# Four layers of convolutions on one core: scan additions that wait for one engine alone, sums for two batches in one GpSimd instruction, two blocks of columns assembled ahead of a turn

## The chip, the cores and the metric

The kernel runs on one core of one Trainium2 chip. The metric is device time in microseconds (us) of one execution; lower is better. The core has TensorE (matmul), VectorE, ScalarE and GpSimd for computing and SyncE (SP), whose queue issues nearly all DMA transfers of this kernel; the profile calls them PE, DVE, ACT, POOL and SP. Each engine works through a queue of its own, and they meet through semaphores.

## The reference

The input is 4 batches of 48 channels of 256 x 256 float32. Four layers follow, each normalized by groups before and added to its input after. The first two (an attention with 3 x 3 convolutions, and a gated convolution) are not touched by the change. Layers 2 and 3 are the scans:

```python
def step(w, b):
    def f(carry, inp):
        nxt = inp + _conv1d(carry, w, b)   # 48 x 48 channels, 5 taps
        return (nxt, nxt)
    return f
# down over the rows, up over the results of down, then
# right over the columns of that, left over the results of right
_, d_rest = jax.lax.scan(step(down_w, down_b), d0, xs[1:])
_, u_rest = jax.lax.scan(step(down_w, down_b), u0, seq)
_, r_rest = jax.lax.scan(step(right_w, right_b), r0, ws[1:])
_, l_rest = jax.lax.scan(step(left_w, left_b), l0, R[Ww - 2::-1])
...
x = x + _L2_conv_ref(_gn(x), ...)
x = x + _L3_conv_ref(_gn(x), ...)
```

Every row or column needs the one before it, so a scan is a chain of 256 steps, and a layer has four of them.

## The kernel before, in words

The function `scans` holds both layers. The four batches are two pairs, and each pair is a **chain** (a Python generator, `chain(pair)`), which runs layer 2 and then layer 3 through down, up, right and left. A row or column of a pair lies on 96 partitions (2 neighbouring places of 48 channels) with 2 batches of 128 numbers, so that the 5 taps become 3 matmuls of 96 x 96 by 96 x 128.

A **step** (L1035 and after) takes the two batches in turn. For each it issues 3 float32 matmuls from the old carry into a bank of PSUM (L1045; the trace records each matmul as two), then one VectorE addition of the bank and the step's input into the new carry (L1049, or L1053 where the input is in one piece), and then calls `keep` for that batch. There are four carry buffers per chain, used in turn; a buffer is written again four steps after its last use. What `keep` does depends on the pass:

- down (L1127) and up (L1168): ScalarE writes the carry with a bias over the input row, in its place;
- right (L1248): ScalarE writes the carry with a bias into the buffer `lines`;
- left (L1293): GpSimd adds the carry to `stage`, which holds the layer's input, so that `stage` becomes the layer's output. In the last left pass of all (layer 3 of chain 1, called `direct`) GpSimd writes the sum into `done` (L1297) in the output's own layout, and SP's queue writes that out (L1316).

Rows are held in tiles of 32 (`RT`), columns in blocks of 16 (`CB`). Large buffers (`slot`) come from a ring of five per pair. While a tile is worked on, the next one is loaded; four ScalarE instructions (L1104, "norms") normalize it in the second half of a tile of the down pass. Results of down and of right go to DRAM (`D`, `Rt`) and come back for up and left; results of up go to `U` by rows and come back by columns (`col`). In right, GpSimd copies a column out of `col` into `pre` (`fetch`, L1225) three steps ahead. The first block of columns is needed as soon as the up pass ends, so it is assembled by hand: its rows from the older tiles are loaded from `U` (L1158) when the up pass is 24 rows into its last tile, and the newest rows are copied straight from the row buffers (L1180) and from `last` (L1192). The second block is loaded from `U` in one transfer (L1235) at the first step of right.

In left of layer 2, statistics for the next normalization are taken from each finished `stage` by eight VectorE instructions (L1325), which the source spreads over the next block's steps.

The order of the work is set by the generators: chain 0 runs alone for LEAD = 992 steps (most of its layer 2), then the chains take turns step by step until chain 0 ends, then chain 1 runs alone. A framework records the instructions, takes each engine's order from the recorded priorities and from its own estimate of when an instruction becomes ready, and adds the semaphore waits that the data need. A wait that an engine has already made, or a later one on the same semaphore, is not made again. An instruction with several waits gets instructions ahead of it that only wait; they show in the profile as EVENT_SEMAPHORE.

When chain 0 has ended, `to_rows(0)` brings its output from the scans' layout into that of the result while chain 1 runs alone: loads (`oi`), four copies for each of 16 halves of a block (`oo`, three on GpSimd at L1393 and one on ScalarE at L1395) and a write. The list `times` says at which of chain 1's steps each piece is issued.

Of the kernel before, what the change touches and what calls it, by code (L numbers as in the profile page):

```python
# [9 lines left out]
F32 = mybir.dt.float32  # L10
# [954 lines left out]
def scans(ctx, tc, xs, out, wts, biases, dram, k, coefs, lead, spare):  # L965
# [49 lines left out]
    def chain(pair):  # L1015
# [66 lines left out]
        def layer_of(layer, first):  # L1082
# [32 lines left out]
            for n in range(NT):  # L1115
                ahead_ = None
                for r in range(RT):
                    if r == 0 and n + 1 < NT:
                        ahead_ = [slot("dn"), slot("dn")]
                        load_rows(layer, n + 1, ahead_, 0, NK)  # L1120
                    if ahead_ and r >= RT // 2 and r % 4 == 0:
# [17 lines left out]


            nc.scalar.activation(last, inner(), AF.Identity, bias=bias[:, 0:1])
            column = None
            for n in reversed(range(NT)):
                ahead_ = None
                for r in reversed(range(RT)):
                    if r == RT - 1 and n > 0:
                        ahead_ = [slot("up"), slot("up")]
                        for i in range(2):
                            nc.sync.dma_start(ahead_[i], D[n - 1][i])
                    if n == 0 and r == RT // 4:  # L1150

                        column = slot("col")
                        v = cols_view(column)
                        for par in range(2):
                            for b in range(2):
                                h0 = NH + 1 - par
                                here = slice(par * C, (par + 1) * C)
                                nc.sync.dma_start(  # L1158
                                    v[here, b, :, h0:, :].rearrange("c q h w -> c q (h w)"),
                                    U[here, b, 0:2, h0:, :].rearrange("c q h w -> c q (h w)"),  # L1160
                                )
# [12 lines left out]
                    yield  # L1174
                    if n == 0 and r < 2:

                        par, h0 = 1 - r, r
                        v = cols_view(column)
                        for q in range(2):
                            nc.sync.dma_start(  # L1180
                                v[par * C : (par + 1) * C, :, q, h0 : h0 + NH, :].rearrange("c b h w -> c b (h w)"),
                                rows_view(now[r])[q * C : (q + 1) * C, :, 0].rearrange("c b h w -> c b (h w)"),
                            )
                if n == 0:

                    def keep(new, b):
                        nc.scalar.activation(last[:, b], new[:, b], AF.Identity, bias=bias[:, 1:2])

                    step(layer, 0, blocks(last), keep)
                    yield  # L1190
                    for q in range(2):
                        nc.sync.dma_start(cols_view(column)[0:C, :, q, 0, :], last[q * C : (q + 1) * C, :, 0:KC])  # L1192
                for r in range(2):
                    v = rows_view(now[r])
                    par = 1 - r
# [25 lines left out]
            def fetch(block, n, w):  # L1221
# [3 lines left out]
                nc.gpsimd.tensor_copy(t, cols_view(block)[:, :, w % 2, :, w // 2])  # L1225
                fetched[g] = t

            for w in range(1, 3):
# [36 lines left out]
            if layer == 0:  # L1265
                stats = [wp.tile([P, NK * 4, 6], F32, tag=f"st{pair}{b}", name="st") for b in range(2)]
            following = None

            direct = layer == 1 and pair == NP - 1
            done, width = None, 0
            writes = []
            for n in reversed(range(NK)):
                ahead_ = None
                if direct and n < 2:
                    done, width = take(0, "done").rearrange("p (b n) -> b p n", b=2), CB
                elif direct and n % 2 == 1:
                    done, width = [take(0, "done") for _ in range(2)], 2 * CB
                for w in reversed(range(CB)):  # L1280
                    if w == CB - 1 and n > 0:
                        ahead_ = slot("lines"), slot("stage")
# [7 lines left out]

                    def keep(new, b):
                        if not direct:
                            nc.gpsimd.tensor_add(to[:, b], to[:, b], new[:, b])  # L1293
                            return
                        for i in range(b.start, b.stop):
                            place = done[i].rearrange("p (h w) -> p h w", w=width)[:, :, n * CB % width + w]
                            nc.gpsimd.tensor_add(place, to[:, i], new[:, i])  # L1297

                    if n == NK - 1 and w == CB - 1:
                        keep(inner(), slice(0, 2))  # L1300
                    else:
                        step(layer, 2, line, keep)
                    if late:
                        late.pop(0)()
                    if writes and (w % 4 == 0 if n < 2 else w % 8 == 4):
                        writes.pop(0)()
                    yield
                if not direct:
                    nc.sync.dma_start(block_of(y, n), by_batch(stage))
                elif n * CB % width == 0:  # L1310

                    def write(b, r, done=done, width=width, w0=n * CB):
# [3 lines left out]
                        nc.sync.dma_start(  # L1316
                            at_rows[:, :, r, w0 : w0 + width],
                            done[b][r * C : (r + 1) * C].rearrange("c (h w) -> c h w", w=width),
                        )

                    writes += [lambda b=b, r=r, f=write: f(b, r) for b in range(2) for r in range(2)]
# [44 lines left out]
                    following = got  # L1366
            first = following

    def to_rows(pair):

        y = xs[2][pair]
        nh = SLOT // W
# [1 line left out]
        for n in range(H // 2 // nh):  # L1374
# [10 lines left out]
            for half in range(2):  # L1385
# [21 lines left out]
    while next(chains[0], True) is None:  # L1407
        next(chains[1])

    pieces = to_rows(0)  # L1410
# [129 lines left out]
```

## Time and profile before

| | us |
|---|---|
| median of 3 runs | 9103.32 |
| lowest and highest run | 9092.42 and 9108.16 |
| the profiled execution's own time | 9095.42 |
| its span, first to last instruction | 9093.6 |
| mean granted TensorE clock | 0.982 |

| stage of the profiled execution | from about, us |
|---|---|
| layers 0 and 1 | 0 |
| chain 0 alone: down, up, right of layer 2 | 3543, 3895, 4205 |
| chain 0 alone: left of layer 2 (few steps of chain 1 between) | 4575 |
| both chains: layer 3 of chain 0, layer 2 of chain 1 | 4986 |
| both chains in left | 6980 |
| chain 1 alone: down, up, right of layer 3 | 7640, 8010, 8317 |
| chain 1 alone: left of layer 3, written straight to the output | 8690 |
| last addition; after it only writes | 9049 |

How to read the profile: durations of single instructions are in ns, all else in us. A row of the costliest groups gives the line, engine and operation, output<-inputs by the program's names, shapes and count, then busy time, mean ns of one, and after the second bar the idle time of the engine just before them with what ended it. The table by stretches gives busy time and count for each engine in each stretch, then the granted TensorE clock, the share of the 16 DMA engines and GB/s. The chain of waits lists, in order of time, start, duration and what was worked on.

### The profile page before, as it was taken

To read this page: it belongs to the slowest core of one execution; us is meant where nothing else is said; L and a number is where in the kernel's file an instruction comes from. 1 tells how busy PE (TensorE), PEld (TensorE's weight loads), DVE (VectorE), ACT (ScalarE), POOL (GpSimd) and SP (SyncE) were. 2 spreads that over 40 slices of the span, in tenths; PEclk is the share of its full clock that TensorE was granted. 3 is DMA by queue.
4 is the path that set the end of the run, shared out by engine and by line. 5 is a ranking of instruction groups with operands and counts; after the bars stand their busy time and mean duration, and the time that the engine had idled before them with its cause. 6 is when DMAs were issued, how large, how long until landed. Compare 5 with 4: busy or idle time off the path is not lost.

```text
span 9093.6 us, 162344 instructions
## 1 busy us (share of the span) xinstructions
PE 8711.1 (96%) x62920; PEld 7268.3 (80%) x62920; DVE 3759.8 (41%) x10790; ACT 3489.6 (38%) x7033; POOL 2067.0 (23%) x3855
## 2 busy tenths in 40 slices
PE   6999999999999987999999999999999999999997
PEld 4777777433333345999999999999999999999997
DVE  3332010234555555444455444444445554343443
ACT  0011000123343355755511776665662004665510
POOL 0000000001111120002465000002446773002475
PEclk9999999999999988999999999999999999999998
DMA  7663323467878878655587773656556787888689
GB/s 150 132 135 87 74 59 73 97 136 168 181 171 187 177 165 165 149 133 128 145 211 178 157 147 95 160 129 160 154 152 177 218 227 169 172 183 201 175 173 168
DMA packets 1201990, 1390.61 MB, mean 153 GB/s; under 512 B 285712, under 2 KB 1128208, under 8 KB 1138240
## 3 DMA queue, kind: packets, MB, share of 16 engines
q1 hardware_dynamic: 1201120, 1379.90, 67.3%
q8 instruction: 493, 8.08, 0.4%
q14 instruction: 281, 2.30, 0.1%
q0 software_dynamic: 96, 0.33, 0.0%
HBM read 812.02 MB, written 509.61 MB: 145 GB/s over the span
## 4 chain that ended last, share of the span: by engine, by line
PE 88%; DMA 4%; DVE 3%; ACT 1%; issue 1%; SPq 1%; POOL 1%; DVEq 0%; POOLq 0%; ACTq 0%
PE ps L1045 57%; PE py L581 7%; PE acc L294 6%; PE acc L295 5%; PE acc L296 4%; PE py L590 3%; PE pt L276 1%; DMA stage<-x 1%; DMA tok<-x 1%; PE ph L698 1%; PE pout L868 1%; DMA x<-y 1%; PE ptok L751 1%; ACT x1n L541 1%; DMA sx<-in_x 1%
## 5 line engine op out<-in xcount | busy, mean ns | idle before, releaser
L1045 PE MATMUL ps<-carry,w 96*96 96x128 f32 x48960 | 5496.1, 275 | 75.6 <-DVE carry L1049 29.7
L1045 PEld LDWEIGHTS ps<-carry,w 96*96 96x96 f32 x48960 | 5445.9, 163 | 129.1 <-DVE carry L1053 39.6
L1225 POOL COPY pre<-col 96x256 f32<-96x256 f32 x1020 | 655.1, 644 | 2800.1 <-DMA col<-last 2011.7
L1248 ACT ACTIVATE lines<-carry,b 96x128 f32<-96x128 f32 (+1 forms) x2044 | 817.0, 402 | 618.8 <-DVE carry L1053 615.2
L1127 ACT ACTIVATE dn<-carry,b 96x128 f32<-96x128 f32 (+1 forms) x2044 | 770.1, 398 | 712.0 <-DVE carry L1049 709.2
L1049 DVE TENSOR_TENSOR carry<-ps,dn 96x128 f32<-96x128 f32 x2280 | 654.7, 288 | 900.5 <-PE ps L1045 806.8
L1053 DVE TENSOR_TENSOR carry<-ps,pre 96x128 f32<-96x128 f32 x2040 | 586.1, 287 | 798.7 <-PE ps L1045 544.8
L1168 ACT ACTIVATE up<-carry,b 96x128 f32<-96x128 f32 x1792 | 718.1, 402 | 480.1 <-DVE carry L1049 479.0
L1293 POOL TENSOR_TENSOR stage<-stage,carry 96x128 f32<-96x128 f32 (+1 forms) x1533 | 790.7, 519 | 314.2 <-DVE carry L1053 184.3
L1053 DVE TENSOR_TENSOR carry<-ps,lines 96x128 f32<-96x128 f32 x2040 | 576.2, 286 | 671.8 <-PE ps L1045 636.8
L1049 DVE TENSOR_TENSOR carry<-ps,up 96x128 f32<-96x128 f32 x1792 | 515.8, 288 | 678.9 <-PE ps L1045 667.9
L581 PE MATMUL py<-x1n,wy 128*96 128x512 f32 x1536 | 705.2, 609 | 29.1 <-ACT x1n L541 27.9
L295 PE MATMUL acc<-xs,xt 128*96 128x288 f32 x2048 | 666.4, 407 | 0.0
L294 PE MATMUL acc<-xt 128*96 128x288 f32 x2048 | 665.9, 408 | 0.0
L581 PEld LDWEIGHTS py<-x1n,wy 128*96 128x96 f32 x1536 | 245.2, 166 | 453.4 <-issue 436.1
L261 ACT ACTIVATE xn<-raw,coef 96x2048 f32<-96x2048 f32 x64 | 133.6, 2093 | 985.8 <-PE pt L276 818.2
L296 PE MATMUL acc<-xt,xs 128*96 128x192 f32 x2048 | 501.8, 327 | 0.0
L279 DVE COPY xt<-pt 128x384 f32<-128x384 f32 x256 | 136.5, 554 | 848.1 <-PE pt L276 649.4
L296 PEld LDWEIGHTS acc<-xt,xs 128*96 128x96 f32 x2048 | 332.0, 164 | 154.2 <-issue 1.2
L295 PEld LDWEIGHTS acc<-xs,xt 128*96 128x96 f32 x2048 | 331.8, 164 | 151.0 <-issue 2.0
L604 DVE TENSOR_TENSOR y<-py,t 96x512 f32<-96x512 f32 x256 | 171.4, 678 | 596.8 <-PE py L590 596.8
L590 PE MATMUL py<-x2n,wy 64*96 64x512 f32 x1536 | 363.0, 601 | 0.0
(179 smaller groups left out, 4823.8 us busy)
## 6 DMA issues: line engine op xcount, KB each, us to landing
stage<-x SPq DMA_DIRECT2D x64, 1536.0 KB
dn<-x SPq DMA_DIRECT2D x240, 384.0 KB
col<-U SPq DMA_DIRECT2D x60, 1536.0 KB
R<-lines SPq DMA_DIRECT2D x60, 1536.0 KB
lines<-R SPq DMA_DIRECT2D x60, 1536.0 KB
D<-dn SPq DMA_DIRECT2D x56, 1536.0 KB
up<-D SPq DMA_DIRECT2D x56, 1536.0 KB
U<-up SPq DMA_DIRECT2D x224, 384.0 KB
```

The lines of the kernel that those rows point to most:

```text
L294: nc.tensor.matmul(acc[0], lhsT=xt[:, h + 2, :], rhs=xt[:, here, :], start=first, stop=last)
L295: nc.tensor.matmul(acc[1], lhsT=xt[:, h + 2, :], rhs=xs[:, here, :], start=first, stop=last)
L296: nc.tensor.matmul(acc[2], lhsT=xs[:, h + 2, :], rhs=xt[:, past, :], start=first, stop=last)
L581: nc.tensor.matmul(ps, lhsT=held["w"][0][:, dx], rhs=x1n[:, 2 * c : 2 * c + 2, dx : dx + W], start=dx == 0, stop=False)
L1045: nc.tensor.matmul(ps, lhsT=w_sb[layer][:, way, j, :], rhs=old[:, i, j : j + W // 2], start=j == 0, stop=j == 2)
L1049: nc.vector.tensor_add(new[:, i].rearrange("p (k w) -> p k w", w=KC), ps.rearrange("p (k w) -> p k w", w=KC), inp[:, i])
L1053: nc.vector.tensor_add(new[:, i], ps, inp[:, i])
L1127: nc.scalar.activation(inp[:, b], blocks(new[:, b]), AF.Identity, bias=bias[:, 0:1])
L1168: nc.scalar.activation(place[:, b], blocks(new[:, b]), AF.Identity, bias=bias[:, 1:2])
L1225: nc.gpsimd.tensor_copy(t, cols_view(block)[:, :, w % 2, :, w // 2])
L1248: nc.scalar.activation(line[:, b], new[:, b], AF.Identity, bias=bias[:, 2:3])
L1293: nc.gpsimd.tensor_add(to[:, b], to[:, b], new[:, b])
```

## The change

Four things change, all of them in `scans`.

1. A new helper `look` is called after each step. It keeps the place that `keep` wrote in this step, and when more than three are kept it takes the oldest and has VectorE read one of its numbers into `seen` (in right together with one number of a fetched column). The list is cleared at the start of every tile of down and up, of right and of left. The last left pass does not call it.
2. In left, other than the last left pass, the GpSimd sum is made once for both batches, after the second addition.
3. At the turn from up to right the second block of columns is assembled by hand as the first was: loads from `U`, copies from the row buffers and from `last`, for two blocks each.
4. In the last left pass, blocks 1 and 0 are collected in one pair of `done` buffers like all others and written together, 32 columns wide, where each was written by itself before. In `to_rows`, the fourth copy is on GpSimd for the pieces up to the sixteenth time and on ScalarE after it, and the last eight times move from 508 + 28 i to 530 + 24 i.

```diff
+        seen = wp.tile([P, 1], F32, tag=f"seen{pair}", name="seen")
+        kept = []
+
+        def look(place, fetched=None):
+            kept.append(place)
+            if len(kept) > 3:
+                if fetched is None:
+                    nc.vector.tensor_copy(seen, kept.pop(0))
+                else:
+                    nc.vector.tensor_add(seen, kept.pop(0), fetched)
...
                     else:
                         step(layer, 0, inp, keep)
+                    look(inp[:, 1, 0, 0:1])
...
-                        column = slot("col")
-                        v = cols_view(column)
-                        for par in range(2):
-                            for b in range(2):
...
-                                    U[here, b, 0:2, h0:, :].rearrange("c q h w -> c q (h w)"),
+                        columns = [slot("col") for _ in range(2)]
+                        for j in range(2):
+                            v = cols_view(columns[j])
+                            for par in range(2):
+                                for b in range(2):
...
+                                        U[here, b, 2 * j : 2 * j + 2, h0:, :].rearrange("c q h w -> c q (h w)"),
...
                         step(layer, 0, place, keep)
+                    look(place[:, 1, 0, 0:1])
...
-                    if w == 0 and n + 1 < NK:
+                    if w == 0 and n == 0:
+                        ahead_ = columns[1]
+                    elif w == 0 and n + 1 < NK:
...
                         step(layer, 1, fetched.pop(n * CB + w), keep)
+                    if n + 1 < NK or w + 1 < CB:
+                        look(line[:, 1, 0:1], fetched[n * CB + w + 1][:, 1, 0:1])
...
-                if direct and n < 2:
-                    done, width = take(0, "done").rearrange("p (b n) -> b p n", b=2), CB
-                elif direct and n % 2 == 1:
-                    done, width = [take(0, "done") for _ in range(2)], 2 * CB
+                if direct and n % 2 == 1:
+                    done = [take(0, "done") for _ in range(2)]
...
                         if not direct:
-                            nc.gpsimd.tensor_add(to[:, b], to[:, b], new[:, b])
+                            if b.stop == 2:
+                                nc.gpsimd.tensor_add(to, to, new)
                             return
...
                         step(layer, 2, line, keep)
+                    if not direct:
+                        look(to[:, 1, 0:1])
...
-                    if writes and (w % 4 == 0 if n < 2 else w % 8 == 4):
+                    if writes and w % 8 == 4:
                         writes.pop(0)()
...
-                    if i < 3:
-                        nc.gpsimd.tensor_copy(dst, src)
+                    if engines[i] is nc.scalar:
+                        nc.scalar.copy(dst, src)
                     else:
-                        nc.scalar.copy(dst, src)
+                        engines[i].tensor_copy(dst, src)
...
-    times = [20 + 26 * i for i in range(16)] + [508 + 28 * i for i in range(8)]
+    times = [20 + 26 * i for i in range(16)] + [530 + 24 * i for i in range(8)]
     for i, _ in enumerate(chains[1]):
+        if i == times[16]:
+            engines[3] = nc.scalar
```

In the changed kernel the reads of `look` stand at lines 1035 and 1037, the matmuls at 1060, the additions at 1064 and 1068, and the GpSimd sum of left at 1325.

More of the change, by code (lines that the diff above doesn't have):

```diff
@@ L1120, in layer_of @@
                         load_rows(layer, n + 1, ahead_, 0, NK)
+                    if r == 0:
+                        kept.clear()
                     if ahead_ and r >= RT // 2 and r % 4 == 0:
@@ L1141, in layer_of @@
             nc.scalar.activation(last, inner(), AF.Identity, bias=bias[:, 0:1])
-            column = None
+            columns = None
             for n in reversed(range(NT)):
                 ahead_ = None
+                kept.clear()
                 for r in reversed(range(RT)):
@@ L1150, in layer_of @@
                     if n == 0 and r == RT // 4:
-                        column = slot("col")
-                        v = cols_view(column)
-                        for par in range(2):
-                            for b in range(2):
[L1156 to L1159, printed above, removed]
-                                    U[here, b, 0:2, h0:, :].rearrange("c q h w -> c q (h w)"),
-                                )
+                        columns = [slot("col") for _ in range(2)]
[3 more added lines that the diff above has]
+                                for b in range(2):
+                                    h0 = NH + 1 - par
+                                    here = slice(par * C, (par + 1) * C)
+                                    nc.sync.dma_start(
+                                        v[here, b, :, h0:, :].rearrange("c q h w -> c q (h w)"),
+                                        U[here, b, 2 * j : 2 * j + 2, h0:, :].rearrange("c q h w -> c q (h w)"),
+                                    )
                     i = n * RT + r + 1
@@ L1177, in layer_of @@
                         par, h0 = 1 - r, r
[L1178 to L1183, printed above, removed]
+                        for j in range(2):
+                            v = cols_view(columns[j])
+                            for q in range(2):
+                                nc.sync.dma_start(
+                                    v[par * C : (par + 1) * C, :, q, h0 : h0 + NH, :].rearrange("c b h w -> c b (h w)"),
+                                    rows_view(now[r])[q * C : (q + 1) * C, :, j].rearrange("c b h w -> c b (h w)"),
+                                )
                 if n == 0:
@@ L1190, in layer_of @@
                     yield
-                    for q in range(2):
-                        nc.sync.dma_start(cols_view(column)[0:C, :, q, 0, :], last[q * C : (q + 1) * C, :, 0:KC])
+                    for j in range(2):
+                        for q in range(2):
+                            nc.sync.dma_start(
+                                cols_view(columns[j])[0:C, :, q, 0, :],
+                                last[q * C : (q + 1) * C, :, j * KC : (j + 1) * KC],
+                            )
                 for r in range(2):
@@ L1226, in fetch @@
                 fetched[g] = t
+            kept.clear()
+            column = columns[0]
             for w in range(1, 3):
@@ L1267, in layer_of @@
             following = None
+            kept.clear()
             direct = layer == 1 and pair == NP - 1
-            done, width = None, 0
+            done = None
             writes = []
@@ L1292, in keep @@
                         if not direct:
[L1293 removed]
+                            if b.stop == 2:
+                                nc.gpsimd.tensor_add(to, to, new)
                             return
                         for i in range(b.start, b.stop):
[L1296 removed]
+                            place = done[i].rearrange("p (h w) -> p h w", w=2 * CB)[:, :, n % 2 * CB + w]
                             nc.gpsimd.tensor_add(place, to[:, i], new[:, i])
@@ L1309, in layer_of, with write @@
                     nc.sync.dma_start(block_of(y, n), by_batch(stage))
-                elif n * CB % width == 0:
-                    def write(b, r, done=done, width=width, w0=n * CB):
+                elif n % 2 == 0:
+                    def write(b, r, done=done, w0=n * CB):
                         at_rows = out[(2 * pair + b) * C : (2 * pair + b + 1) * C].rearrange(
@@ L1316, in write @@
                         nc.sync.dma_start(
-                            at_rows[:, :, r, w0 : w0 + width],
-                            done[b][r * C : (r + 1) * C].rearrange("c (h w) -> c h w", w=width),
+                            at_rows[:, :, r, w0 : w0 + 2 * CB],
+                            done[b][r * C : (r + 1) * C].rearrange("c (h w) -> c h w", w=2 * CB),
                         )
@@ L1367, in chain, with to_rows @@
             first = following
-    def to_rows(pair):
+    def to_rows(pair, engines):
         y = xs[2][pair]
@@ L1408, in scans @@
         next(chains[1])
-    pieces = to_rows(0)
-    times = [20 + 26 * i for i in range(16)] + [508 + 28 * i for i in range(8)]
+    engines = [nc.gpsimd] * 4
+    pieces = to_rows(0, engines)
+    times = [20 + 26 * i for i in range(16)] + [530 + 24 * i for i in range(8)]
     for i, _ in enumerate(chains[1]):
+        if i == times[16]:
+            engines[3] = nc.scalar
         if i in times:
```

## The prediction

> **What bounds the kernel now.** I read the page's shares first, then busy time by stage, then the chain of waits at the three places that the diff touches.
>
> ```profile
> PE 8711.1 (96%) x62920; PEld 7268.3 (80%) x62920; DVE 3759.8 (41%) x10790; ACT 3489.6 (38%) x7033; POOL 2067.0 (23%) x3855
> L1045 PE MATMUL ps<-carry,w 96*96 96x128 f32 x48960 | 5496.1, 275 | 75.6 <-DVE carry L1049 29.7 <-DVE carry L1053 28.5 <-ACT carry L1109 10.0
> ```
>
> TensorE bounds it, and 60% of the span is the scans' L1045: 4080 steps of 12 recorded matmuls. Only 75.6 us of idle stands before them, so what can be had lies in the pace of a step.
>
> ```profile
> core 0: us, PE busy (x) PEld busy (x) DVE busy (x) ACT busy (x) POOL busy (x), PEclk, DMA share, GB/s
> 3910.00:4150.00 240.00, 240.00 (x2143) 239.63 (x2142) 102.81 (x357) 143.31 (x358) 0.00 (x0) 1.00 0.61 140
> 4220.00:4560.00 340.00, 340.00 (x2971) 331.39 (x2970) 142.29 (x496) 200.76 (x504) 154.25 (x240) 1.00 0.53 145
> 7000.00:7500.00 500.00, 500.00 (x4571) 500.00 (x4570) 264.40 (x858) 0.00 (x0) 391.44 (x762) 1.00 0.79 219
> ```
>
> These are stretches: chain 0 alone going up, chain 0 alone going right, both chains going left. Time over matmuls, by 12, is a step: 1.344, 1.373 and 1.313 us. With two chains TensorE is full at 1.313. Alone, the loop matmul, addition, matmul is late by 0.03 (down, up) to 0.06 us (right) a step.
>
> The addition's cost is seen on VectorE: L1049 and L1053 hold 8057 EVENT_SEMAPHORE records of 21 ns for 8160 additions: one or two waits ahead of nearly each.
>
> The left pass hands work to GpSimd:
>
> ```profile
> L1293 POOL TENSOR_TENSOR stage<-stage,carry 96x256 f32<-96x256 f32 x3 | 2.6, 856 | 6.2 <-DVE carry L1053 6.2
> ...
> 4640.45 0.30 DVE carry L1053
> 4640.75 0.07 issue
> 4640.82 0.53 POOL stage L1293
> 4641.35 0.02 issue
> 4641.37 0.04 DVE st L1325
> ```
>
> The first row (groups by shape) prices a sum for both batches, as each left pass has one today: 856 ns; one for one batch takes 519. The chain of waits below gives the hand-over: addition's end to GpSimd's start 0.08 us (4640.74 to 4640.82), GpSimd's end to VectorE's start 0.03.
>
> Last, two stalls that GpSimd and DMA make:
>
> ```profile
> POOL pre L1225 <- DMA col<-U: 14.4, 1, 14.4
> ...
> 8351.78 10.86 PE L1045 MATMUL ps<-carry,w 96*96 96x128 f32 x72 [9.73 <-DVE carry L1053]
> ...
> DMA packets 52841, 3.60 MB, mean 81 GB/s; under 512 B 52841, under 2 KB 52841, under 8 KB 52841
> ```
>
> Chain 1's second block of columns is late in layer 1: TensorE idles 9.73 us, then runs at half clock. The third line is the time after the last addition, 9049.4 to 9093.6: 44.2 us of DMA alone, writing two blocks of 16 columns.
>
> **What the Trainium skill says.** "Perfetto Trace Analysis", Identifying Dependency Chains: an instruction that waits on several engines may get EventSemaphore instructions ahead of it. The 8057 records agree. "TensorE: Matmul & The Clock Gate", first table, gives VectorE a strict FIFO queue: what waits at its head holds all behind it. The trace agrees: the statistics at 4641.37 waited for GpSimd and the next addition came at 4641.98. The same page, Part 1, says that idleness throttles the clock; after the 9.73 us gap the granted clock was 0.50 for 5 us more.
>
> **Part 1, reads of a kept number (L1035, L1037).** About 3,600 one-element reads are added, nearly one a step. Such a copy (L89, 96x1) takes 146 ns; statistics of 690 ns let the next addition start after 610, so I take 146-80=about 65 ns of VectorE's queue. In exchange an addition waits for TensorE alone. By the built program's order on VectorE this holds for all but some 70 additions outside chain 1's last left pass, which keeps its waits.
> Gain: alone, a step falls from 1.344 (down, up) and 1.373 (right) toward 1.313. Down and up: 510 steps by 0.03 = 15 us; right: 255 by 0.06 = 15; two chains: 60 us. The loop might stop at 1.32, so I take 56, ends 30 and 62. Where both chains run, nothing is gained: the other chain already covers the wait.
>
> Cost: what a read waits for, since everything later on VectorE's queue stands behind it: the next additions of both chains and the statistics, and TensorE waits for the additions. The source puts the read three steps later, but the order of the built program has them earlier:
> - Down, up: the read of a step stands after the next addition (either chain's). ScalarE's copy ends some 0.45 us after the step's second addition (0.04 to start, 0.40 long); the addition behind the read is due 1.0 us after. Free. Around norms (2081 ns) most reads stand one or two additions later, which covers them.
> - Right: it also reads a fetched column, 0.13 + 0.644 + 0.03 = 0.8 us after. Free by 0.2 us. But 12 copies to rows (1126 ns) fall among fetches on GpSimd, each then holding VectorE up to 0.9 us, where three steps of slack hid it: +10 us, ends 0 and 20.
> - Left, except chain 1's last: in 591 of 759 steps the read stands directly behind its own step's second addition and waits for GpSimd's sum of that very step. So VectorE stands for 0.08 + 0.856 + 0.03 = 0.97 us, where the next addition was due 0.37 us after.
>
> **Left, both chains** (some 205 pairs of steps). VectorE per chain's step: first addition to second 0.19 (as at 4641.98, two in 0.47), second 0.28, stand 0.97, read 0.065: 1.505 us. Two in turn: 3.01 against 2.63 of TensorE. VectorE becomes the bound: 0.39 x 205 = +80 us, ends 45 and 105 (if a tile's last and first steps, where statistics stand between, keep today's pace, 160 pairs).
>
> **Left, chain 0 alone** (16 tiles). Now a tile of 16 steps takes 23.57 us (from the chain's starts 4620.72, 4644.29), 1.354 a step plus a stall at the statistics. After: addition to addition 1.51, and the second waits for a matmul that started late (start to addition 1.01, at 4659.33 to 4660.34): steps alternate between 1.5 and 1.78, mean 1.64. Ten such make 16.4; the six around the eight statistics (0.61 each on the queue, one waiting 0.97) some 10.5. Sum 26.9: +3.3 a tile, +53 us, ends 20 and 65.
>
> **Part 2, one sum for both batches.** GpSimd spends 856 where it spent two times 519, but starts only after the second addition. Its saving lies beside other work; its delay is in the 0.97 above.
>
> **Part 3, two blocks of columns early.** Per transition four more col<-U, four more col<-up and two more col<-last go through SP's queue (0.3 to 0.6 us each, some 5), ahead of the U writes; one 1536 KB load goes. Of these, the two for the first step may add 1 us. Removed: 9.7 us of idle and about 5 us at half clock worth 2.6. The third block's load now follows; it has 16 steps, 21 us, and needs 15. Gain 13 minus small, ends 4 and 16; at the other three transitions no such stall stands, so nothing.
>
> **Part 4, last writes.** Blocks 1 and 0 leave as one, in runs of 128 B instead of 64. A block is 4 writes of 48 x 128 runs, 24,576 packets; the tail above moved 52,841 in 44.2 us at 98% of 16 engines, so 13.1 ns each (44.2 x 0.978 x 16 / 52,841), that is both blocks and some 3,700 packets of 128 B. After: 24,576 and about as many queued before, 28,300 x 13.1 / 16 = 23 us, with the landing 24, if a run of 128 B takes no longer than one of 64. Gain 20, and 2 earlier, where stage loads wait behind the writes: 22, ends 12 and 28. Moving the fourth copy to GpSimd (16 halves, of which ten move) and later start times: ScalarE loses ten copies of 1117 ns in stretches where additions waited for it 1.2 us: 0.
>
> **Sum** on the profiled execution (span 9093.6, own time 9095.4): +80 +53 +10 -56 -13 -22 = +52: 9147. It stands 7.9 below the median, 9103.3: I predict 9155.
>
> **Rivals.**
> *Faster.* The reads never hold: GpSimd's sum would have to end within 0.37 us of the second addition. Then 10-56-13-22 = -81: about 9022. For: with two chains each has a whole step of the other, 1.313 us, as cover, and GpSimd is at 78% there. Against: 856 ns measured, three times, and both chains' reads stand in one queue, so that their waits add up. It decides at a stand of 0.78 us in the left passes with both chains (1.505 becomes 1.313): below that they cost nothing.
> *No difference.* The left costs are at their lower ends (45+20), with gains whole (-91): 9103 - 16 = 9087.
> *Much slower.* Gaps in TensorE's work bring the half clock into the left passes, and the reads in right miss their 0.2 us (512 steps alone by 0.1 = +50): about 9230.
> *It does not do what it says:* the additions would still show extra waits; the built order speaks against it except in the last pass.
>
> **Numbers.** My case (left passes pay more than the rest brings) 0.65, faster rival 0.15, no difference 0.12, much slower 0.08. About 0.2%, 18 us, is what a measurement can tell from no change. Faster by more 0.16, within 0.12, slower 0.72. The range 9070 to 9240 takes in the low end of the second rival and the much slower case, and leaves most of the faster one out.
>
> **What would show it.** In the changed profile: two-chain left stretches at about 3.0 us a pair with fewer matmuls than 4571 in 500 us, and VectorE waiting there at L1035 for POOL; down, up and right alone at 1.31 to 1.32 a step; EVENT_SEMAPHORE records on VectorE at additions down to a few hundred; no gap near the last right pass's second block; a tail near 24 us. Left passes at 1.313 with reads that wait for nothing would prove me wrong.

## The result, and the profile after

The change makes the kernel slower: 9130.22 us median (9123.01 to 9145.44, 6 runs) against 9102.86 us of the kernel before in the same comparison; the ratio is 1.0033 with a 95% interval of 1.002 to 1.0046. In microseconds that is +27 by the medians, +30 by the ratio and +32.5 by the two profiled spans (9126.1 against 9093.6). Behind the small number stand two large ones: some 135 us lost in the left passes and some 100 us gained elsewhere.

First the page's shares of the changed kernel (busy us, share of the span, instructions):

```profile
PE 8752.7 (96%) x62920; PEld 7227.1 (79%) x62920; DVE 4048.3 (44%) x14409; ACT 3475.7 (38%) x7023; POOL 1946.7 (21%) x3100
```

VectorE has 3619 instructions more, GpSimd 755 fewer; TensorE's share is still 96%. The shares don't tell where the time went. The table by stretches does. Its rows here are chain 0 alone going up, chain 0 alone going right, both chains going left, and chain 1 alone going up; the columns are those of the table in the prediction.

```profile
3910.00:4130.00 220.00, 220.00 (x2013) 220.00 (x2012) 105.54 (x489) 134.54 (x335) 0.00 (x0) 1.00 0.58 139
4200.00:4510.00 310.00, 309.94 (x2830) 309.44 (x2829) 172.04 (x708) 189.24 (x472) 151.88 (x236) 1.00 0.57 155
7100.00:7600.00 500.00, 494.72 (x3962) 441.49 (x3961) 225.94 (x1070) 0.00 (x0) 281.97 (x331) 1.00 0.71 192
8110.00:8370.00 260.00, 260.00 (x2373) 259.50 (x2372) 124.60 (x575) 160.14 (x397) 19.49 (x18) 1.00 0.85 195
```

Twelve recorded matmuls are a step. One chain alone now takes 1.311 us (up), 1.314 (right) and 1.315 (chain 1, up), where it took 1.344 and 1.373: the pace of two chains. But in left the third row has 3962 matmuls in 500 us where 4571 stood before: 3.03 us for a pair of steps instead of 2.63. TensorE still shows 494.72 of 500 us busy (the ends of matmuls are modelled); the count of matmuls and the weight loads, busy for 441.49 us where they had been for all 500, give it away. The granted clock is 1.00, so nothing was slowed by the throttle.

The groups by shape and the list of waits name the reason. After the second bar stands the idle time ahead of the group; in the list of waits come total us, times and the longest.

```profile
L1325 POOL TENSOR_TENSOR stage<-stage,carry 96x256 f32<-96x256 f32 x768 | 656.5, 855 | 592.6 <-DVE carry L1068 554.7 <-DVE seen L1035 18.2 <-issue 15.3
...
L1035 DVE COPY seen<-stage 96x1 f32<-96x1 f32 x759 | 111.9, 149 | 597.4 <-POOL stage L1325 594.0
```

```profile
DVE seen L1035 <- POOL stage L1325: 594.0, 650, 1.4
```

VectorE stood still for 594 us ahead of 650 of the 759 one-number reads in left, waiting for GpSimd's sums, and GpSimd stood 554.7 us ahead of the sums, waiting for VectorE's additions: they work in turn. The timeline (start, duration, engine and line, then the idle before it and what ended it) shows one turn, with both chains going left:

```profile
7300.57 0.15 DVE L1035 COPY seen<-stage 96x1 f32<-96x1 f32 x1 [0.97 <-POOL stage L1325]
7300.65 0.48 DVE L1068 TENSOR_TENSOR carry<-ps,lines 96x128 f32<-96x128 f32 x2
...
7301.20 0.85 POOL L1325 TENSOR_TENSOR stage<-stage,carry 96x256 f32<-96x256 f32 x1 [0.66 <-DVE carry L1068]
7302.09 0.15 DVE L1035 COPY seen<-stage 96x1 f32<-96x1 f32 x1 [0.97 <-POOL stage L1325]
```

Two additions back to back (both halves had been waiting in PSUM), 0.07 us to GpSimd, 0.85 for the sum, 0.04 back to the read, then the next two additions 0.08 us after the read's start: 1.52 us per chain's step here, and two chains in turn.

Two places that should have improved did. The mid-pass stall of chain 1's last right pass is gone; what is left there is a gap of 6.23 us before its first step (timeline of TensorE), where the kernel before had 4.0:

```profile
8389.86 15.38 PE L1060 MATMUL ps<-carry,w 96*96 96x128 f32 x112 [6.23 <-DVE carry L1282]
```

And after the last addition (9093.3 us) the writes move fewer and larger packets; this is the transfers' line for that stretch:

```profile
DMA packets 31058, 3.96 MB, mean 121 GB/s; under 512 B 31058, under 2 KB 31058, under 8 KB 31058
```

31,058 packets instead of 52,841, but the tail fell only from 44.9 to 32.8 us.

### The profile page after: what moved, and what is told of

The parts are those of the page before. It is cut to its first block, busy times and chain, and to the rows that moved or that the text cites. A ratio compares the mean times of both kernels' runs of the same rounds, so it can differ in the third digit from the quotient of the medians.

```text
span 9126.1 us, 159207 instructions
## 1 busy us (share of the span) xinstructions
PE 8752.7 (96%) x62920; PEld 7227.1 (79%) x62920; DVE 4048.3 (44%) x14409; ACT 3475.7 (38%) x7023; POOL 1946.7 (21%) x3100
## 5 line engine op out<-in xcount | busy, mean ns | idle before, releaser
L1325 POOL TENSOR_TENSOR stage<-stage,carry 96x256 f32<-96x256 f32 x768 | 656.5, 855 | 592.6 <-DVE carry L1068 554.7
L1068 DVE TENSOR_TENSOR carry<-ps,lines 96x128 f32<-96x128 f32 x2040 | 535.2, 280 | 238.1 <-PE ps L1060 195.8
L1035 DVE COPY seen<-stage 96x1 f32<-96x1 f32 x759 | 111.9, 149 | 597.4 <-POOL stage L1325 594.0
```

The source lines that it names most:

```text
L1068: nc.vector.tensor_add(new[:, i], ps, inp[:, i])
L1325: nc.gpsimd.tensor_add(to, to, new)
```

## The experiments

Two theories were set against each other. **A, the place of the read**: in 591 of 759 steps the read stands in VectorE's queue directly behind its own step's second addition, so it holds everything for GpSimd's sum of that very step. **B, the one large sum** that left now makes is the cost, whoever waits for it. **C**, a third, is the mere number of reads. Each run below is compared with the kernel before on the same chip.

**left_no_read.** No read in left.

```diff
-                    if not direct:
-                        look(to[:, 1, 0:1])
```

> The changed kernel without the reads in left; left keeps its one GpSimd sum a step, and its additions wait for GpSimd themselves again, four steps back. Theory A (the cost is the place of the read: it stands directly behind its own step's second addition in VectorE's queue and holds every later instruction for the 0.85 us sum and two hand-overs, a cycle of 1.51 us a chain step): both-left returns to 2.63 us a pair (at the 8000 of additions where the changed kernel is 91 us behind, it is then at about -28), left alone returns to about 1.47 us a step, whole kernel about 9015 us (9000 to 9030). Rival B (the one large sum is the cost, whoever waits for it): still 9110 to 9140, both-left near 3.0 us a pair. Rival C (it is the reads as extra VectorE instructions, wherever they stand, some 0.065 us each): 759 reads x 0.065 = 49 us off at most, about 9080.

Measured: 8992.1 us, ratio 0.9887 (0.9873 to 0.99). The stretch with both chains in left:

```profile
7000.00:7480.00 480.00, 480.00 (x4391) 480.00 (x4390) 252.74 (x819) 0.00 (x0) 311.91 (x367) 1.00 0.81 224
```

4391 matmuls in 480 us are 2.624 us a pair, with the one large sum still there. B falls, and C, which could give back 49 us at most. The reads in left alone cost 1.0033 / 0.9887, or 1.5%, some 135 us. The expectation was 23 us too high, because the other parts brought more than I had counted: 103 us by this ratio, where the prediction's terms for them give 81 (below).

**left_two_sums.** Two GpSimd sums a step again, reads as they were.

```diff
-                            if b.stop == 2:
-                                nc.gpsimd.tensor_add(to, to, new)
+                            nc.gpsimd.tensor_add(to[:, b], to[:, b], new[:, b])
```

> The changed kernel with two GpSimd sums a step in left, as before the change; the reads stay where they were, directly behind their step's second addition. Theory A: with both halves ready, a chain step's cycle on VectorE and GpSimd is 0.08 read + 0.24 first addition + 0.07 hand-over + two sums of 0.52 one after the other + 0.04 back = 1.47 us, against 1.51 with the one sum; a little shorter when the halves arrive apart. So both-left 2.9 us a pair (not 2.63), left alone about 1.5 instead of 1.64 us a step, and the whole 20 to 45 us shorter: about 9090 us (9060 to 9115). Rival B (GpSimd's load or the one large sum): one-sum is the cheaper on GpSimd (855 against 2 x 519 ns), so if load counts 9150 or more; if the large sum is what is wrong, about 9015. Rival C (number of reads): 9130, no change.

Measured: 9074.4 us, ratio 0.9978 (0.9972 to 0.9985). Its timeline with both chains in left:

```profile
7301.72 0.15 DVE L1035 COPY seen<-stage 96x1 f32<-96x1 f32 x1 [0.91 <-POOL stage L1324]
7301.79 0.47 DVE L1068 TENSOR_TENSOR carry<-ps,lines 96x128 f32<-96x128 f32 x2
7302.15 0.99 POOL L1324 TENSOR_TENSOR stage<-stage,carry 96x128 f32<-96x128 f32 x2 [0.46 <-DVE carry L1068]
...
7303.17 0.15 DVE L1035 COPY seen<-stage 96x1 f32<-96x1 f32 x1 [0.91 <-POOL stage L1324]
```

1.45 us a chain's step, 2.93 a pair from 7000 to 7550 us (4511 matmuls). GpSimd works longer (0.99 us for the two) and yet the kernel is faster, since the first sum starts before the second addition has ended (7302.15 against 7302.26), and the read's stand falls from 0.97 to 0.91 us. What counts here is the time from the second addition to the read's release. Theory A gave 2.9 and a gain of 20 to 45 us; it was 50 by the two ratios, a little more than expected, and by the traces about 22 of it came where both chains go left and 27 in chain 0's first left pass.

**one_sum_only.** The kernel before with the one large sum alone.

```diff
-                            nc.gpsimd.tensor_add(to[:, b], to[:, b], new[:, b])
+                            if b.stop == 2:
+                                nc.gpsimd.tensor_add(to, to, new)
```

> The kernel before with nothing changed but left's two GpSimd sums of a step put into one. No reads. Theory A: the additions wait for a sum of four steps back, which is long done; within 10 us of the kernel before, about 9103 us. Rival B (the one large sum costs): slower by 50 to 100 us, 9150 to 9200. Rival C: no change, 9103.

Measured: 9095.3 us, ratio 1.0 (0.9992 to 1.0008). Where only additions four steps later and the statistics wait for it, the large sum makes no difference that this run can tell; the interval leaves room for some 7 us either way. One small cost shows in the traces: in chain 0's first left pass VectorE's statistics stood 20.0 us waiting for GpSimd instead of 15.0, and the pass took 378.6 us instead of 374.8.

**left_late_read.** The read is tied to a later carry, so that it stands two steps of its chain after the addition whose sum it waits for.

```diff
-                        look(to[:, 1, 0:1])
+                        look(to[:, 1, 0:1], carry[at[0] - 1][:, 1, 1:2])
```

> The changed kernel, but left's read takes the element of the kept sum and, as second operand, one element of the carry of the step before the present one, so that it can't stand earlier in VectorE's queue than that: 4 of the chain's own halves after the addition whose sum it waits for (8 halves with both chains running), where it stood 0 after it. Same number of reads, same one sum. Theory A: the sum is done 2 chain steps earlier, no wait is left at the read; both-left 2.63 us a pair, left alone 1.35 to 1.4 us a step, whole kernel about 9005 us (8990 to 9020), a little better than without reads in left. Rival B (the one large sum): about 9130. Rival C (the reads' own number): about 9130.

Measured: 9069.2 us, ratio 0.997 (0.9959 to 0.9981): a clear miss, more than half of the loss was still there. The wait had gone, but the reads themselves had grown; this is the list of the line's instructions (minimum, median and maximum ns), and then the timeline in left with chain 0 nearly alone:

```profile
L1037 DVE TENSOR_TENSOR seen<-stage,carry x759: 93/835/855, 4533.7 to 7677.4; 96x1 f32<-96x1 f32 x190
```

```profile
4700.26 0.85 POOL L1325 TENSOR_TENSOR stage<-stage,carry 96x256 f32<-96x256 f32 x1 [0.89 <-DVE carry L1068]
4700.28 0.84 DVE L1037 TENSOR_TENSOR seen<-stage,carry 96x1 f32<-96x1 f32 x1
4701.05 0.47 DVE L1068 TENSOR_TENSOR carry<-ps,lines 96x128 f32<-96x128 f32 x2
```

A sum of two single numbers (on each of the 96 partitions) takes 0.84 us, and it ends 10 ns after GpSimd's sum beside it, which it did not ask for. 722 of the 759 reads began while such a sum ran. The Trainium skill, "SBUF — State Buffer", Who interferes with whom, says that a VectorE instruction with two SBUF inputs contends with a GpSimd instruction that reads SBUF, and that the one that comes second is blocked for the whole of the other. These records agree: the reads that began during a sum took 835 ns (median), the 39 others 156.

**left_late_scalar.** The same place in the queue, but the second number is a scalar operand, so that one SBUF tensor is left.

```diff
-        def look(place, fetched=None):
+        def look(place, fetched=None, op=nc.vector.tensor_add):
...
-                    nc.vector.tensor_add(seen, kept.pop(0), fetched)
+                    op(seen, kept.pop(0), fetched)
...
-                        look(to[:, 1, 0:1])
+                        look(to[:, 1, 0:1], carry[at[0] - 1][:, 1, 1:2], nc.vector.tensor_scalar_add)
```

> The changed kernel with left's read placed late, as in left_late_read, but of another form: the kept element is the one tensor operand and the carry's element a scalar operand, where left_late_read had two tensor operands. In left_late_read 722 of the 759 reads began while GpSimd's sum was running and ended 10 ns (median) after that sum, with a median of 835 ns for one element, though the sum that they asked for was long done. Theory A[...] (a VectorE instruction with two SBUF tensors doesn't run beside a GpSimd sum; one with a single SBUF tensor does, as the 140 ns copies in left of the changed kernel did in the 42 cases in which they met a sum): reads of 0.14 to 0.2 us, both-left 2.63 us a pair, left alone 1.33 to 1.4 us a step, whole kernel about 8975 us (8955 to 8995). Rival (the wait is still for the wrong sum, whatever the form): as left_late_read, about 9070. Rival (a late read holds the additions in some other way): between the two, with a wait of VectorE for POOL at the read.

Measured: 8988.8 us, ratio 0.988 (0.9865 to 0.9895). Timeline, same part of the pass:

```profile
4700.33 0.85 POOL L1325 TENSOR_TENSOR stage<-stage,carry 96x256 f32<-96x256 f32 x1 [0.46 <-DVE carry L1068]
4700.36 0.21 DVE L1037 TENSOR_SCALAR seen<-stage,carry 96x1 f32<-96x1 f32 x1
4700.62 0.29 DVE L1068 TENSOR_TENSOR carry<-ps,lines 96x128 f32<-96x128 f32 x1
```

The read starts beside the sum and takes 0.21 us; the next addition starts at 4700.62, when the sum still runs. Both chains: 2.624 us a pair (4299 matmuls in 470 us). So the form of the late read was the second cause, and the place of the early one the first. Against no reads at all, reads that hold nothing bring no difference that these runs can tell (8988.8 and 8992.1, intervals overlap): chain 0's first left pass takes 371.1 us instead of 382.8, but the last left of all takes 360.5 instead of 355.2.

**late_direct_scalar.** left_late_scalar with such reads in the last left pass too, taken from `done`.

```diff
-                    if not direct:
-                        look(to[:, 1, 0:1])
+                    mark = to[:, 1, 0:1]
+                    if direct:
+                        mark = done[1].rearrange("p (h w) -> p h w", w=2 * CB)[:, 0:1, n % 2 * CB + w]
+                    look(mark, carry[at[0] - 1][:, 1, 1:2], nc.vector.tensor_scalar_add)
```

> left_late_scalar with such reads also in the last left, whose additions wait for GpSimd themselves in all other kernels. Its 256 steps take 355 us in the changed kernel, 1.39 a step, against 1.31 in down, up and right with reads. If the additions' own wait for GpSimd is what is left there, 1.33 a step: 10 to 18 us less than left_late_scalar, about 8960 us. Rival (GpSimd's two or more sums a step, or the transfers, set this stage): within 4 us of left_late_scalar.

Measured: 8993.0 us, ratio 0.9887 (0.9874 to 0.9901): no gain. The list of waits in the last left pass:

```profile
POOL done L1329 <- DMA stage<-x: 38.4, 7, 7.6
DVE seen L1037 <- POOL done L1329: 20.9, 18, 3.8
```

GpSimd waits for the input's loads, seven times, and VectorE through it.

**late_direct_scalar_one_x** and **left_late_scalar_one_x.** late_direct_scalar and left_late_scalar without the last left pass's loads of the input but for the first; all 16 blocks of sums are then added to that one block, so these two show times alone.

```diff
-                        ahead_ = slot("lines"), slot("stage")
+                        ahead_ = slot("lines"), stage if direct else slot("stage")
                         nc.sync.dma_start(ahead_[0], Rt[n - 1])
-                        nc.sync.dma_start(by_batch(ahead_[1]), block_of(x, n - 1))
+                        if not direct:
+                            nc.sync.dma_start(by_batch(ahead_[1]), block_of(x, n - 1))
```

> late_direct_scalar with the last left's loads of the input x left out but for the first block (all its 16 blocks of columns are added to that one block, so these outputs are not the reference's). If the transfers set the last left (GpSimd's last sums waited 38 us for stage<-x in late_direct_scalar, and the share of DMA was 1.02), its 256 steps take 336 to 340 us instead of 361, and the whole is 20 to 30 us shorter: about 8967 us. Rival (GpSimd's two sums a step or the additions set it): within 5 us of 8993.

> left_late_scalar with the same loads left out: the last left without reads. With the transfers out of the way, what its additions' own wait for GpSimd costs shows: if 1.39 a step is theirs, 355 us for the 256 steps, and 12 to 20 us more than late_direct_scalar_one_x (about 8983 us). Rival (only the transfers set it): within 4 us of late_direct_scalar_one_x.

Measured: 8964.0 us, ratio 0.9848 (0.9834 to 0.9861), and 8969.3 us, ratio 0.9859 (0.9844 to 0.9874). The last left takes 334.5 us with reads and 344.5 without, where both took 360.5. So the loads of the input lengthen that pass by 16 to 26 us once the rest is fast. That they are also what gives back part of left_late_scalar's gain is not shown: its last left took 360.5 us, four other kernels with the same last left took 354.0 to 355.6, and there is one trace of each. What the additions' own waits cost there is 10 us by the traces, less than the 12 to 20 expected, and the two runs' intervals overlap.

Three runs, each the kernel before with one part alone, price what the other parts bring. **reads_rows_only** has `look` in down, up and right, and not in left.

```diff
+                    look(inp[:, 1, 0, 0:1])
...
+                    look(place[:, 1, 0, 0:1])
...
+                    if n + 1 < NK or w + 1 < CB:
+                        look(line[:, 1, 0:1], fetched[n * CB + w + 1][:, 1, 0:1])
...
```

> The kernel before with the reads in down, up and right alone: none in left, two sums a step in left, columns and last writes as before. The prediction's term for this is -56 us (-30 to -62). From the traces of before and after, chain by chain alone: down -15 and -16, up -7 and -9, right about -9 twice, and -9 where chain 0 starts the second layer: -55 to -70, so about 9035 us (9025 to 9050). Rival (what these stages gained in the changed kernel came with the other parts, not with the reads): 9080 or more.

Measured: 9034.0 us, ratio 0.9933 (0.992 to 0.9945), -61 us.

**columns_only** has part 3.

```diff
-                        column = slot("col")
+                        columns = [slot("col") for _ in range(2)]
...
-                    if w == 0 and n + 1 < NK:
+                    if w == 0 and n == 0:
+                        ahead_ = columns[1]
+                    elif w == 0 and n + 1 < NK:
...
```

> The kernel before with the two early blocks of columns alone. The prediction's term is -13 us (-4 to -16), from the gap at the second block of the last right. About 9084 us (9080 to 9094) if the gap goes. Rival (the gap is only moved: the start of right now waits longer, for 8 assembling transfers instead of 4): 9094 to 9100.

Measured: 9077.7 us, ratio 0.998 (0.9973 to 0.9988), -18 us.

**last_writes_only** has the wide last write of part 4.

```diff
-                if direct and n < 2:
-                    done, width = take(0, "done").rearrange("p (b n) -> b p n", b=2), CB
-                elif direct and n % 2 == 1:
-                    done, width = [take(0, "done") for _ in range(2)], 2 * CB
+                if direct and n % 2 == 1:
+                    done = [take(0, "done") for _ in range(2)]
...
-                    if writes and (w % 4 == 0 if n < 2 else w % 8 == 4):
+                    if writes and w % 8 == 4:
...
```

> The kernel before with the last two blocks' sums kept together and written in pieces of 128 bytes, and nothing else. The prediction's term is -20 us (-12 to -28) net of what it adds; the tail after the last addition went only from 44.9 to 32.8 us in the changed kernel. Theory (that difference is the whole worth): -12, about 9084 us (9078 to 9090). Rival (the packets' number alone sets the tail, and the changed kernel's tail was longer for another reason): -20 or more, 9076 or less. Rival (the transfers only come later): 9095.

Measured: 9089.7 us, ratio 0.9989 (0.9983 to 0.9996), -9 us; in the traces the last addition is at 9048.7 in both and the tail is 33.9 instead of 44.9. Of the three expectations the first holds, the second's lower edge is passed by 2, and the third sides with -12, not -20.

One line of reads_rows_only, from the waits of chain 1's last right pass, shows that two parts help each other:

```profile
DVE seen L1037 <- POOL pre L1245: 39.0, 109, 12.9
```

With the late second block still there, a read waits 12.9 us for it, where the addition had idled TensorE for 9.73: the read looks one column ahead and meets the late block earlier. That pass takes 364.9 us before, 362.4 with reads alone, 352.7 with columns alone, and 342.9 in left_no_read, which has both: 7 us more than the two singly.

## Why the prediction was right

The forecast was 9155 us, slower, and 9130 was measured. By its own steps:

| term | predicted, us | shown, us |
|---|---|---|
| left, both chains | +80 | +83, and +10 where one of the two goes left |
| left, chain 0 alone | +53 | +42 |
| right's reads behind copies to rows | +10 | about +7.5, by another mechanism |
| reads, one chain alone | -56 | -61 together with the line above |
| columns | -13 | -18 |
| last writes | -22 | -9 |
| one sum for two batches | 0 | 0 |

**Left, both chains.** The 1.505 us from queue order and durations was right to 0.01: 3.026 us a pair against 2.624 in left_no_read, over 207.5 pairs, is 83 us. The stand was 0.97 us as worked out. Left out were the stretches at both ends, 46 and 40 pairs, in which only one chain goes left; they lost 0.08 and 0.15 us a pair, 10 us in all.

**Left, chain 0 alone.** The pass took 426.2 us, 26.6 a tile (26.9 predicted) against 374.8 before: +51, as forecast. But not all of it is the reads' doing. Compared with left_no_read, which runs the same steps up to the turn into layer 3, the loss is 42 us to chain 0's first addition there: the term was too large by about 11. The other 9 us stand in left_no_read too, whose pass took 382.8 us without a read: chain 1 does more of its early steps in it (37 additions instead of 30), which the count for chain 0 alone left out, and the one large sum alone made it 378.6.

Together the two left terms came to 135 us where 133 was forecast. That this fits so well is luck: one was 13 too small, the other 11 too large.

**Rows and right.** The step's floor of 1.31 was reached, a little lower than the 1.32 that I allowed for, and right as well. Before the cost of the next paragraph is taken off, the reads brought some 68 us where 56 was forecast.

The copies to rows cost nearly what the term says, but not in the way it says. It had the reads wait for fetches that stand behind the copies in GpSimd's queue. The timeline of left_no_read, in chain 1's last right pass, has the fetch done before the read starts:

```profile
8349.48 0.64 POOL L1251 COPY pre<-col 96x256 f32<-96x256 f32 x1 [0.67 <-DVE carry L1068]
...
8350.07 1.12 POOL L1430 COPY oo<-oi 96x1024 f32<-96x1024 f32 x1
8350.16 1.03 DVE L1037 TENSOR_TENSOR seen<-lines,pre 96x1 f32<-96x1 f32 x1 [0.15 <-POOL pre L1251]
```

The fetch ends at 8350.12. The read, which takes two SBUF numbers, starts at 8350.16 beside a copy to rows and ends with it at 8351.19. Ten of the twelve copies had such a read beside them; these took 0.65 to 1.04 us each, where 0.156 is usual, and all ten ended within 0.02 us of their copy. The trace of the changed kernel has the same ten. So the hold that left_late_read showed was in the changed kernel from the start, in right. The eleven steps around these reads took 7.5 us more than 1.312 each. (The pass took 342.9 us against 334.3 in chain 0's right pass without copies; the gap at its start lies ahead of the first addition and is not in these.) So the number came near by luck. A read of one SBUF number in right, which would test this, had no run.

**Columns.** The step that failed is "at the other three transitions no such stall stands, so nothing". Chain 0's first turn did have the stall: one of its first steps in right took 20.67 us. It was filled with 15 steps of chain 1 (14 to 29 done while chain 0 went right), so TensorE showed no idle. In columns_only no such step is left, chain 1 takes none of its steps there and some 26 instead of 14 in the turn into layer 3, and by the additions done, about 8 us are won at that turn. A stall filled with borrowed steps is not free. The term for the last right pass held: 364.9 us before and 352.7 in columns_only, 12 of the 13.

**Last writes.** The tail was to be 24 us; it was 33. Of the sum, the packets were 31,058 for 28,300, and each took 13.9 ns of an engine (32.7 us x 82.3% busy x 16 / 31,058), not 13.1: that is 27 us. The remaining 6 are time in which the DMA engines were not all busy, the share being 82.3% and not the 97.8% taken from the tail before; what left them idle is open.

**The sum.** The shown parts add up to about +47; +30 was measured. Of the difference, 7 us are the joint gain of reads and columns; some 10 remain, within the intervals of five ratios, or with the moved copies of `to_rows`, which had no run of their own. That is open.

**Of the rivals**, the faster one asked for a stand under 0.78 us; it was 0.97, and left_two_sums at 0.91 still pays. The half clock of the much slower one did not come: it stayed at 1.00 in left. The change also does what it says: EVENT_SEMAPHORE records at the additions fell from 8057 to 850. The changed kernel without reads in left, or with late reads of one tensor there, is 1.1 to 1.2% faster than the kernel before, and those are the versions to use.

## What to carry to other kernels

An instruction put into a queue to take waits away from others makes everything behind it wait, so its worth is decided by its place in the built order relative to the producer, not by its place in the source; work out the cycle from the producer's end to the release, and compare it with the time in which the bound engine needs its next input. Its form counts too: the reads of two SBUF numbers were held here by GpSimd's sums and copies beside them, those of one were not. Price parts by runs of their own: here a gain of about 100 us was hidden under a loss of 135. A stall that another chain's steps fill still costs those steps later.

## What the runs showed of the hardware

A VectorE addition of two single numbers in SBUF took 0.835 us (median) instead of 0.156 when a GpSimd sum of two SBUF tensors was running, and ended with it. In right, ten such additions were held in the same way by GpSimd copies of 1.12 us. A copy of one number took 0.14 us (28 that began during a sum in the changed kernel) and a scalar-operand addition 0.21 beside the same sum, and the scan's additions, which take one operand from PSUM, kept their 0.27 to 0.29 us. In the last writes, runs of 128 bytes took 13.9 ns of a DMA engine each where runs of 64 took 13.1.
